# Cross-attention with layer norm: three score tiles in two TensorE visits, and a new order of the work

## Chip, core and metric

The kernel runs on one core of a Trainium2 chip. The metric is the device time of one execution in microseconds (us). A core has five engines with a queue of instructions each: TensorE (PE in the profile, with its weight loads as PEld), VectorE (DVE), ScalarE (ACT), GpSimd (POOL) and SyncE (SP), which here only issues DMA transfers.

## What is computed

Four batches of 2048 rows attend over 77 context rows each; 16 heads of 32 columns; then an output projection, a residual and a layer norm:

```
qs = (q @ wq).reshape(Bq, Lq, H, HD).transpose(0, 2, 1, 3)
ks_ = (k @ wk).reshape(Bq, Lk, H, HD).transpose(0, 2, 1, 3)
vs = (v @ wv).reshape(Bq, Lk, H, HD).transpose(0, 2, 1, 3)
scores = jnp.einsum('bhqd,bhkd->bhqk', qs, ks_) / jnp.sqrt(jnp.float32(HD))
scores = jnp.where(mask[:, None, :, :], -jnp.inf, scores)
attn_w = jax.nn.softmax(scores, axis=-1)
attn = jnp.einsum('bhqk,bhkd->bhqd', attn_w, vs)
out = attn @ wo + q
mu = jnp.mean(out, axis=-1, keepdims=True)
var = jnp.mean((out - mu) ** 2, axis=-1, keepdims=True)
return (out - mu) / jnp.sqrt(var + EPS) * gamma + beta
```

D is 512, everything is float32. q is x (8192 rows in all), k and v are the context.

## The kernel before

The 8192 rows are 64 tiles of 128 rows; two tiles make a block, four make a group. The steps of a tile, with the letter that the order uses for each:

- Q, q: one quarter of a group's query projection (12 matmuls of 512 columns, `pq`, line 177) and its copy out of PSUM (DVE, `q`, line 194). Inputs come by g (load), i (ACT cast) and j (POOL split into a high and a low part).
- S: the scores of one tile (`sc`, line 309). A head has 32 rows of contraction, so four heads run side by side in the array, and two halves of the rows too. That is 32 matmuls, which the profile shows as 64 instructions. Head h = 4g + j writes to the bank of its j, so a tile fills four PSUM banks with four blocks of 77 scores each.
- T: the maxima, in four parts of four heads. One DVE instruction for each head adds the mask, reduces and writes the negated scores to `pbuf` (line 324). Three `pbuf` take turns.
- e: the exponentials on ACT, one instruction for each head (line 339), also in four parts.
- r, n: reciprocal of the sums (DVE, line 345) and normalising (POOL, line 350).
- t: transpose in 32 x 32 blocks (DVE, line 373). P: twelve DMA transfers for each block that regroup the transposed rows, `B` to `PT` (line 385).
- V: attention of a block (`pa`, line 419); a, b: its split into a high part (ACT, line 468) and a low part (DVE, line 472).
- O: output projection of a tile (12 matmuls, `po`, line 517), + the residual (DVE, line 520), s the moments (DVE, lines 525 and 530, and on POOL the factors, lines 534 to 537), k scaling (ACT, line 543), f gamma and beta (POOL, lines 547 and 548), x and w the load of x and the store of the result.
- Once in 16 tiles: the mask of the next batch (load_mask, mask_bias, mask_min, mask_nan, lines 279 to 296).

PSUM has eight banks. They are handed out in turn (`bank`), so an instruction that writes to a bank waits until the last reader of what was there eight banks before has finished.

Nothing schedules the work: each engine runs its instructions as they are written. For tiles 0 to 53 a loop over pairs of tiles writes them. In one turn u it does S(u), O(u-6), a Q, V of block u/2-2, S(u+1), O(u-5) and another Q; from tile 54 on the words of `ORDER` are carried out one by one by `do`.

Of the kernel before, what the change touches and what calls it, by code (L numbers as in the profile page):

```python
# [8 lines left out]
F32 = mybir.dt.float32  # L9
# [4 lines left out]
ALU = mybir.AluOpType  # L14
# [3 lines left out]
P = 128  # L18
D = 512
H = 16  # L20
HD = 32
NK = 77
# [4 lines left out]
GH = 4  # L27
NG = H // GH
HEADS = [GH * g + j for j in range(GH) for g in range(NG)]
NC_D = D // P  # L30
BLK = 256
GRP = 2 * BLK
# [4 lines left out]
KSCALE = 1.0 / HD**0.5  # L37
LATE = 48
CUT = 27
HALVES = [slice(0, D // 2), slice(D // 2, D)]  # L40

ORDER = """
S54 T54.3 i31 e54.3 T54.0 O49 q58 e54.0 k47 T54.2 T54.1 +49 t53 S55 T55.0 T55.1 Q59 f47 x50 x52 T55.3 e54.2 T55.2
e54.1 j31 r54 n54 O48 q59 s49 P26.9s +48 S56 e55.0 P26.4s e55.2 e55.1 e55.3 T56.1 T56.0 P26.6g P26.0s V25 T56.2 x51
r55 a25.0 a25.1 t54 e56.1 S57 e56.2 T56.3 T57.2 Q62 P26.2g P26.8s n55 e56.3 T57.1 Q60 t55 u49 b25.0 e56.0 P26.3g Q63
e57.1 p49 e57.2 T57.3 T57.0 r56 w47 s48 b25.1 P26.5s x59 e57.3 x53 S58 P26.10s P26.7g P27.7g q62 e57.0 k46 n56 q60  # L50
P27.0s q63 u48 p48 T58.1 T58.2 P26.1s P27.1s P26.11s T58.3 e58.1 r57 t56 P27.11s n57 Q61 P27.6s f46 e58.2 T58.0 V26
q61 a26.1 t57 a26.0 x55 f48 e58.0 S59 P27.2s T59.2 P27.5s e58.3 T59.3 e59.3 P27.3s P28.4g P27.8s T59.0 O51 b26.0
P28.11g T59.1 P27.9s +51 P28.6g r58 e59.2 P28.5g O50 P27.10s b26.1 s51 e59.1 P27.4s n58 S60 Y0 u51 +50 P28.0s x57
e59.0 P28.7g P28.10s V27 T60.0 T60.1 a27.0 T60.2 a27.1 T60.3 e60.1 r59 t58 w46 P28.3s P28.9s S61 n59 O52 P28.1s
e60.3 b27.0 s50 T61.0 T61.3 t59 f49 u50 e61.0 e61.3 T61.2 b27.1 T61.1 O53 P28.8s P29.1g P29.9g e61.2 O54 S62 +52
e61.1 +53 s52 x54 r61 P28.2s V28 +54 P29.7g e60.2 x62 T62.1 T62.2 O55 p50 n61 e60.0 T62.3 x56 P29.4s r60 n60 T62.0
t61 v51 M0 P29.8s a28.0 a28.1 b28.1 b28.0 f50 t60 +55 O57 e62.2 P29.6s e62.1 P29.5s P29.10s +57 P30.6g P29.3s
P29.11s k51 P29.2s P29.0s P30.10s P30.1s e62.0 e62.3 u52 v52 S63 V29 P30.2s T63.0 P30.9s P30.5g s53 P30.7g P30.11a
s55 T63.1 r62 a29.1 P30.4s T63.3 P30.0s e63.0 P30.3s n62 b29.1 T63.2 O56 a29.0 b29.0 e63.1 I54 u53 e63.3 P30.8s s57
h63.0 y55 t62 +56 f51 O59 u55 e63.2 x58 O58 x60 k52 m63.0 y54 V30 h63.1 m63.1 I56 U62.7s U62.6s +59 J56 a30.1 u56  # L60
U62.4s U62.8s R63.0 U62.9s x61 U62.11s s59 y57 a30.0 u57 +58 u59 b30.1 b30.0 U62.5s z57 R63.1 y53 J54 R63.3 U62.1s
U62.0a R63.2 w48 E63.0a f52 w51 s58 U62.10s O60 U62.3s +60 w50 O61 U62.2a w52 y58 X63 M1 z53 E63.1a v56 v59 s60 z55
+61 y60 E63.2a u54 W62 u58 k56 E63.3a w49 w57 u60 z54 k59 c62 w54 I61 J61 W63 f56 z58 c63 d62 y61 w53 z60 w55 u61
f59 O62 w56 d63 z61 +62 s62 y62 w58 w61 w59 O63 u62 s63 z62 w60 y63 u63 w62 z63 w63
"""


# [1 line left out]
def xattn_layernorm(  # L69
# [26 lines left out]
    ring, kept, rows, summed = [], set(), {}, set()  # L96

    def bank(name):
        while len(ring) % 8 in kept:
# [196 lines left out]
        nc.vector.tensor_scalar(nz, nz, 0.0, EPS, ALU.mult, ALU.add)  # L296


    def scores(t):
        qs = qd[t // 4]  # L300
        nmax[t] = sb.tile([P, H], F32, tag="nm", bufs=3, name=f"nm_{t}")
        sums[t] = sb.tile([P, H], F32, tag="sum", bufs=3, name=f"sum_{t}")
        sc = scs[t] = [bank(f"sc_{t}_{j}") for j in range(GH)]
        for g in range(NG):
            for half in range(0, P, P // 2):
                for j in range(GH):
                    q = slice(HD * j, HD * (j + 1))
                    r0 = (t % 4) * P + half
                    nc.tensor.matmul(  # L309
                        sc[j][half : half + P // 2, g * NK : (g + 1) * NK],  # L310
                        qs[q, g, r0 : r0 + P // 2],
                        kct[q, g, t // TPB, keys_of(j)],
                        start=True,
                        stop=True,
                    )

    def maxima(t, lo, hi):
        pb = pbuf[t % NPB]
        mb = bat[t // TPB][0]
        nm = nmax[t]  # L320
        for h in HEADS[lo:hi]:
            g, j = divmod(h, GH)
            i = slot(h)
            nc.vector.tensor_tensor_reduce(  # L324
                pb[:, i // 2, (i % 2) * NK : (i % 2 + 1) * NK],
                scs[t][j][:, g * NK : (g + 1) * NK],
                mb[:, t % TPB, keys_of(h)],
                -1.0,
                3.0e38,
                ALU.add,  # L330
                ALU.min,
                accum_out=nm[:, i : i + 1],
            )

    def exps(t, lo, hi):
        pb = pbuf[t % NPB]
        for i in map(slot, HEADS[lo:hi]):
            p = pb[:, i // 2, (i % 2) * NK : (i % 2 + 1) * NK]
            nc.scalar.activation(  # L339
                p, p, AF.Exp, bias=nmax[t][:, i : i + 1], scale=-1.0, accum_out=sums[t][:, i : i + 1]  # L340
            )
# [180 lines left out]
    def moments(t):  # L522
        b, tt = divmod(t, 2)
        st = sb.tile([P, 6], F32, tag="st", bufs=3, name=f"st_{t}")
        nc.vector.bn_stats(st, od[t])
        if tt == 0:
            mvs[b] = sb.tile([P, 2, 2], F32, tag="mv", bufs=3, name=f"mv_{b}")
            rns[b] = sb.tile([P, 2, 2], F32, tag="rn", bufs=3, name=f"rn_{b}")
        mv, rn = mvs[b], rns[b]
        nc.vector.bn_aggr(mv[:, tt, :], st)  # L530
        nz = bat[t // TPB][1]
        if tt == 1:
            k = (t - 1) % TPB
            nc.gpsimd.tensor_tensor(rn[:, 0, :], mv[:, :, 1], nz[:, k : k + 2], ALU.add)
            nc.gpsimd.tensor_tensor(rn[:, 0, :], rn[:, 0, :], mhalf, ALU.pow)
            nc.gpsimd.tensor_tensor(rn[:, 1, :], mv[:, :, 0], rn[:, 0, :], ALU.mult)
            nc.gpsimd.tensor_tensor(rn[:, 1, :], rn[:, 1, :], mneg, ALU.mult)

    def scale(t):
        o = od[t]  # L540
# [170 lines left out]
        return casts.get(u) or [((u + 8) // 4, u % 4)] * (u + 8 < 4 * NGRP)  # L711

    evac = [(0, 0)]
    for u in range(0, 2 * CUT, 2):
        n = u // 2
        m, k = divmod(u, TPB)

        for q in pieces(u + 2):
            if u >= 4:
                load_xT(*q)  # L720
# [52 lines left out]
        if k == TPB - 6 and m + 1 < NB:  # L773
            load_mask(m + 1)
        if k == TPB - 4 and m + 1 < NB:
            mask_bias(m + 1)
        if k == TPB - 2 and m + 1 < NB:
            mask_min(m + 1)
            mask_nan(m + 1)

        if u:
            recip(u)
# [38 lines left out]
            q_visit(*q)  # L821
        if u >= 5:
            moments(u - 5)
        if u:
            recip(u + 1)
            normalise(u + 1)
# [5 lines left out]


    tile_ops = {
        "S": scores, "r": recip, "n": normalise, "t": transp, "W": av_tile, "x": load_x, "X": resid, "O": o_proj,
        "+": residual, "u": rsqrt_one, "y": centre, "z": finish, "k": scale, "f": affine, "w": store,
        "v": bias_one, "K": stretch, "G": shift, "p": pool_scale, "I": act_mean, "J": act_squares, "M": keep,
    }
    tile_parts = {"T": maxima, "e": exps}
    visits = {"Q": q_visit, "q": q_evac}  # L840
# [3 lines left out]
    def do(op, k, part=0, queue="s"):  # L844
        if op == "k" and k >= LATE:
            scale_one(k)
        elif op == "z" and k == NT - 1:
            finish_last(k)
        elif op == "w" and k == NT - 1:
            od.pop(k)  # L850
        elif op in tile_ops:
            tile_ops[op](k)
        elif op in tile_parts:
            tile_parts[op](k, q4 * part, q4 * part + q4)
        elif op == "s":
            (moments_one if k >= LATE else moments)(k)
        elif op in "hm":
            (recip_half if op == "h" else normalise_half)(k, part)
        elif op in visits:
            visits[op](*divmod(k, 4))  # L860
        elif op in inputs:
            inputs[op](k // 2, k % 2 * 2)
        elif op == "P":
            regroup_part(k, part, by[queue])
        elif op == "U":
            regroup_tile(k, part, by[queue])
        elif op == "R":
            flip(k, part)
        elif op == "E":
            flip_evac(k, part, nc.vector.tensor_copy if queue == "v" else nc.scalar.copy)  # L870
        elif op == "Y":
            turn_values()
        elif op == "V":
            av(k)
        elif op in "ab":
            (av_hi if op == "a" else av_lo)(k, part)
        else:
            (av_hi if op == "c" else av_lo)(k // 2, k % 2, True)

    for word in ORDER.split():  # L880
        op, (k, part) = word[0], (word[1:] + ".").split(".")[:2]
# [50 lines left out]
```

## Time and profile before

| | |
|---|---|
| median of 3 runs | 513.45 us (512.91 to 514.86) |
| profiled execution | 512.54 us, of which the span of the profile is 510.7 us |
| granted TensorE clock | 0.996 |
| busy share of the span | PE 98%, DVE 92%, ACT 92%, POOL 83% |
| DMA | 109.34 MB, mean 214 GB/s |

A row of a group gives busy time and the mean of one instruction; a row of a timeline gives start, length, engine, line, operation, output<-inputs, shape, and how many alike follow each other. Matmuls are pipelined, so starts tell more than lengths. A row of a stretch gives its length, then for each engine the busy time and how many instructions were under way.

### The profile page before, as it was taken

What the parts mean: (1) busy time and instruction counts of PE and PEld (TensorE: products, weight loads), DVE (VectorE), ACT (ScalarE), POOL (GpSimd) and SP (SyncE); (2) the same over time, 40 slices, a digit from 0 to 9 for tenths busy, and PEclk for the clock granted to TensorE, in tenths of its full rate; (3) what the DMA queues carried; (4) which work ended last, traced back from release to release, by engine and by line L of the source; (5) the groups of instructions that cost most, each with busy time, mean ns of one, the idle gap of its engine ahead of it and who ended that gap; (6) DMA issues with size and microseconds to landing.
All of it is one profiled execution on the core that took longest, in us unless ns stands there. A gap on an engine that the chain in (4) does not pass through costs nothing.

```text
span 510.7 us, 20467 instructions
## 1 busy us (share of the span) xinstructions
PE 502.1 (98%) x6864; PEld 387.3 (76%) x6864; DVE 472.1 (92%) x2574; ACT 471.2 (92%) x2239; POOL 424.3 (83%) x382
## 2 busy tenths in 40 slices
PE   8999999999999999999999999999999999999994
PEld 6987777777777777777777777777777777777784
DVE  6798999899999888989999898889999989999997
ACT  6798999999899999999899999999899999999861
POOL 0659359988799988888989998898889989999894
PEclk9999999999999999999999999999999999999998
DMA  8946867888777888789777897788887778767665
GB/s 304 400 155 150 224 177 197 217 237 221 189 207 201 233 215 224 193 222 246 185 202 218 228 230 192 181 235 230 223 217 192 211 198 234 192 185 216 166 207 207
DMA packets 58280, 109.34 MB, mean 214 GB/s; under 512 B 9203, under 2 KB 10739, under 8 KB 58176
## 3 DMA queue, kind: packets, MB, share of 16 engines
q1 hardware_dynamic: 55776, 103.19, 73.1%
q0 software_dynamic: 1872, 4.20, 2.9%
q8 instruction: 55, 0.90, 0.8%
q10 hardware_dynamic: 528, 0.66, 0.4%
q14 instruction: 49, 0.40, 0.3%
HBM read 41.53 MB, written 16.78 MB: 114 GB/s over the span
## 4 chain that ended last, share of the span: by engine, by line
PE 87%; DVE 5%; DMA 4%; SPq 2%; POOL 1%; issue 1%; ACT 1%; DVEq 0%; POOLq 0%
PE pq L177 30%; PE po L517 29%; PE pa L419 10%; PE sc L309 10%; PE sc L517 3%; DMA PT<-B 2%; DVE B L373 2%; PE pv L243 2%; PE pk L203 1%; SPq L385 1%; DVE pbuf L324 1%; DMA stage_a<-wq 1%; PE pq L669 1%; POOL pbuf L350 0%; DVE q L194 0%
## 5 line engine op out<-in xcount | busy, mean ns | idle before, releaser
L339 ACT ACTIVATE pbuf<-pbuf,nm 128x77 f32<-128x77 f32 x1024 | 352.5, 350 | 15.0 <-DVE nm L324 13.6
L339 ACT ACTIVATION_READ_ACCUMULATOR pbuf<-pbuf,nm 128x1 f32 x1024 | 195.3, 191 | 0.0
L324 DVE CUSTOM_DVE_ANT_0 pbuf<-sc,mb 128x77 f32<-128x77 f32 x1020 | 169.9, 230 | 21.8 <-PE sc L309 21.5
L350 POOL TENSOR_TENSOR pbuf<-pbuf,ri 128x1232 f32<-128x1232 f32 x63 | 142.2, 2258 | 17.8 <-DVE ri L345 11.0
L177 PE MATMUL pq<-xth,wqh 128*128 128x512 f32 (+1 forms) x256 | 98.8, 386 | 0.0
L177 PE MATMUL pq<-xtl,wqh 128*128 128x512 f32 (+1 forms) x256 | 98.0, 383 | 0.0
L177 PE MATMUL pq<-xth,wql 128*128 128x512 f32 (+1 forms) x256 | 97.9, 383 | 0.0
L373 DVE STREAM_TRANSPOSE B<-pbuf 128x1280 f32<-128x1280 f32 x63 | 93.9, 1491 | 0.3
L517 PE MATMUL po<-woh,AH 128*128 128x512 f32 x224 | 93.3, 416 | 0.0
L517 PE MATMUL po<-wol,AH 128*128 128x512 f32 x224 | 87.7, 391 | 0.0
L517 PE MATMUL po<-woh,AL 128*128 128x512 f32 x224 | 86.7, 391 | 0.0
L324 DVE DVE_READ_ACCUMULATOR2_ANT nm<- 128x1 f32 x1024 | 83.2, 81 | 0.0
L547 POOL TENSOR_TENSOR o<-o,gam 128x512 f32<-128x512 f32 x53 | 69.9, 1319 | 14.4 <-ACT o L543 14.4
L548 POOL TENSOR_TENSOR o<-o,bet 128x512 f32<-128x512 f32 x53 | 68.4, 1290 | 4.2
L309 PEld LDWEIGHTS sc<-kct,q 32*64 32x64 f32 x4080 | 51.2, 130 | 23.7 <-issue 21.3
L170 POOL TENSOR_TENSOR xtl<-xtf,xth 128x1024 fp32r<-128x1024 f32 x28 | 67.1, 2398 | 0.0
L309 PE MATMUL sc<-kct,q 32*64 32x77 f32 x4080 | 61.2, 238 | 0.0
L419 PE MATMUL pa<-PT,vsb 96*32 96x256 f32 x960 | 58.2, 382 | 0.7 <-DMA PT<-B 0.3
L177 PEld LDWEIGHTS pq<-xth,wqh 128*128 128x128 f32 x256 | 48.1, 188 | 9.8
L177 PEld LDWEIGHTS pq<-xth,wql 128*128 128x128 f32 x256 | 48.1, 188 | 9.4
L177 PEld LDWEIGHTS pq<-xtl,wqh 128*128 128x128 f32 x256 | 48.1, 188 | 9.1
L517 PEld LDWEIGHTS po<-woh,AH 128*128 128x128 f32 x224 | 42.0, 188 | 12.0 <-DVE nm L324 0.4
(167 smaller groups left out, 707.5 us busy)
## 6 DMA issues: line engine op xcount, KB each, us to landing
PT<-B SPq DMA_DIRECT2D x355, 128.0 KB
xtf<-xT SPq DMA_DIRECT2D x28, 512.0 KB
o<-x SPq DMA_DIRECT2D x56, 256.0 KB
out<-o SPq DMA_DIRECT2D x56, 256.0 KB
PT<-B POOLq DMA_DIRECT2D x16, 128.0 KB, 5.2
o_end<-x SPq DMA_DIRECT2D x7, 256.0 KB
out<-o_end SPq DMA_DIRECT2D x7, 256.0 KB
xtf<-xT SPq DMA_DIRECT2D x4, 256.0 KB
```

The lines of the kernel that those rows point to most:

```text
L170: nc.gpsimd.tensor_tensor(l, fx.pop((g, c)), h.bitcast(F32), ALU.subtract)
L177: nc.tensor.matmul(pq, w[:, c, m * P : (m + 1) * P], r[:, c, rs], start=(n == 0), stop=(n == 11))
L243: nc.tensor.matmul(pv, ctx_s[c][i][:, r, :], v[c], start=(n == 0), stop=(n == 11))
L309: nc.tensor.matmul(sc[j][half : half + P // 2, g * NK : (g + 1) * NK], qs[q, g, r0 : r0 + P // 2], kct[q, g, t // TPB, keys_of(j)], start= ...
L324: nc.vector.tensor_tensor_reduce(pb[:, i // 2, (i % 2) * NK : (i % 2 + 1) * NK], scs[t][j][:, g * NK : (g + 1) * NK], mb[:, t % TPB, keys_ ...
L339: nc.scalar.activation(p, p, AF.Exp, bias=nmax[t][:, i : i + 1], scale=-1.0, accum_out=sums[t][:, i : i + 1])
L350: nc.gpsimd.tensor_tensor(pv, pv, rv.to_broadcast((P, NP, 2, NK)), ALU.mult)
L373: nc.vector.transpose(bt.rearrange("p c q r -> p q c r"), pbuf[t % NPB].rearrange("p q (c r) -> p q c r", c=5),)
L419: nc.tensor.matmul(pas[b, g // 2][HD * j : HD * (j + 1), (g % 2) * BLK : (g % 2 + 1) * BLK], vsb[:, 2 * b // TPB, HD * h : HD * (h + 1)], ...
L517: nc.tensor.matmul(pos[t][:, cols], a[:, c, rs], w[:, c, cols], start=go, stop=done)
L547: nc.gpsimd.tensor_tensor(o, o, gam, ALU.mult)
L548: nc.gpsimd.tensor_tensor(o, o, bet, ALU.add)
```

## The change

1. From tile 12 to tile 59 the scores of three tiles (48 heads) are computed in two TensorE visits of 24 heads (Z, `scores_shared`). A visit fills four banks with six blocks of 77 scores each. Three tiles so take 8 banks and not 12.
2. The middle tile of three has its four groups of columns in two visits, so its maxima and exponentials go through the heads in another order (`SHARED`).
3. The loop ends after tile 11. From there to tile 53 the words of `STEADY` are repeated every six tiles. A word `e0.2:0:2` is: operation, tile (or visit, block, quarter) counted within six, how many repeats it lags behind, and the first repeat. The last ten tiles have a new `ORDER`. Transfers P stand apart in the order, exponentials and maxima of neighbouring tiles are mixed.
4. The POOL part of the moments becomes an operation of its own (N, `factors`), and the mask of the next batch is made after the last maxima of an odd tile (`next_mask`).

```diff
-    def scores(t):
-        qs = qd[t // 4]
-        sc = scs[t] = [bank(f"sc_{t}_{j}") for j in range(GH)]
-        for g in range(NG):
-            for half in range(0, P, P // 2):
...
+    def score_rows(cells, sc):
+        for n, (t, g) in enumerate(cells):
+            for j in range(GH):
+                scs[t, g * GH + j] = sc[j][:, n * NK : (n + 1) * NK]
             for half in range(0, P, P // 2):
                 for j in range(GH):
+                    score(t, g * GH + j, half)
+
+    def scores(t):
+        score_rows([(t, g) for g in range(NG)], [bank(f"sc_{t}_{j}") for j in range(GH)])
+
+    def scores_shared(v):
+
+        cells = [(v // 2 * 3 + n // NG, n % NG) for n in range(3 * NG)]
+        shared.add(v // 2 * 3 + 1)
+        score_rows(cells[v % 2 * 6 : v % 2 * 6 + 6], [bank(f"sz_{v}_{j}") for j in range(GH)])
+
+    def heads_of(t, lo, hi):
+        return (SHARED if t in shared else HEADS)[lo:hi]
...
-    for u in range(0, 2 * CUT, 2):
+    for u in range(0, 2 * MERGE, 2):
...
+STEADY = """
+Z0:0:2 Q1:-1:3 T0.2:0:2 T1.0:0:2 T0.1:0:2 O4:2:1 T0.0:0:2 Z1:0:2 e0.2:0:2 T1.1:0:2 i0:-2:4 Q0:-1:3 t5:1:1 e0.1:0:2
...
+    for n in range(STEADY_FROM, STEADY_TO):
+        for e, lag, first in steady:
+            b = n - lag
+            op, (k, part) = e[0], (e[1:] + ".").split(".")[:2]
+            period = 4 if op == "Z" else 3 if op in "PVabgij" else 6
+            k = int(k) + period * b
+            if b < first or k >= NT * period // 6:
+                continue
+            do(op, k, int(part or 0))
+            if op == "T" and k % 2 and part == "3":
+                next_mask(k - 1)
```

TensorE goes through the big operations of six tiles in this order: Z, Q, O, Z, Q, O, O, V, Z, O, Q, Q, O, Z, V, O, Q, Q, V, and then the next Z. Here is what stands on TensorE before the scores of tile 24 in the kernel before (`sc_24_0` to `sc_24_3` are its four banks, `pq` a query projection):

```order
L177 MATMUL pq_7_0_3472<-xtl_7_3016,wqh_67 128x512
L177 MATMUL pq_7_0_3472<-xth_7_3015,wql_68 128x512
L309 MATMUL sc_24_0_3505<-kct_71,q_6_2928 64x77
L309 MATMUL sc_24_1_3506<-kct_71,q_6_2928 64x77
L309 MATMUL sc_24_2_3507<-kct_71,q_6_2928 64x77
L309 MATMUL sc_24_3_3508<-kct_71,q_6_2928 64x77
```

And in the changed one, where `sz_16` is the visit with tile 24 and half of tile 25, and `pa_9` the attention of block 9:

```order
L198 MATMUL pq_7_1_3322<-xtl_7_2589,wqh_67 128x512
L198 MATMUL pq_7_1_3322<-xth_7_2588,wql_68 128x512
L468 MATMUL pa_9_0_3405<-PT_9_3231,vsb_72 32x256 x8
L468 MATMUL pa_9_1_3406<-PT_9_3231,vsb_72 32x256 x8
L324 MATMUL sz_16_0_3467<-kct_71,q_6_2713 64x77
L324 MATMUL sz_16_1_3468<-kct_71,q_6_2713 64x77
L324 MATMUL sz_16_2_3469<-kct_71,q_6_2713 64x77
L324 MATMUL sz_16_3_3470<-kct_71,q_6_2713 64x77
```

The attention has moved in between the projection and the scores; the visit then has 48 matmuls, not 32.

On SP, the transfers around the regrouping of blocks 14 and 15 in the kernel before (`PT_14` is block 14, `out` a store, `o_28<-x` a load of x, `xtf` a load of input):

```order
L385 DMA PT_14_4430<-B_14_4291 32x2x512 x12
L551 DMA out<-o_22_3771 128x512
L551 DMA out<-o_23_3773 128x512
L161 DMA xtf_10_2_4592<-xT 128x1024
L489 DMA o_28_4594<-x 128x512
L489 DMA o_29_4596<-x 128x512
L385 DMA PT_15_4706<-B_15_4564 32x2x512 x12
```

And in the changed one:

```order
L434 DMA PT_14_4530<-B_14_4244 32x2x512 x3
L538 DMA o_27_4704<-x 128x512
L434 DMA PT_14_4530<-B_14_4244 32x2x512 x5
L538 DMA o_26_4790<-x 128x512
L434 DMA PT_14_4530<-B_14_4244 32x2x512 x4
L434 DMA PT_15_4853<-B_15_4585 32x2x512 x5
L601 DMA out<-o_23_4251 128x512
L434 DMA PT_15_4853<-B_15_4585 32x2x512 x2
L601 DMA out<-o_21_3894 128x512
L434 DMA PT_15_4853<-B_15_4585 32x2x512 x5
```

The twelve transfers of a block stand in pieces now, with loads and stores between them; block 15 is the first of a group of three.

On ACT, before, around the split of block 11's attention (`AH_11`; `sum_27` are exponentials of tile 27, `xth` a cast of input, `o_18<-o_18` a scaling):

```order
L543 ACTIVATE o_18_3228<-o_18_3228,rn_9_3608 128x512
L543 ACTIVATE o_19_3230<-o_19_3230,rn_9_3608 128x512
L468 CAST AH_11_3923<-pa_11_0_3905 128x512
L468 CAST AH_11_3923<-pa_11_1_3906 128x512
L339 ACTIVATE pbuf0_77,sum_27_3928<-pbuf0_77,nm_27_3927 128x77 x16
L166 CAST xth_9_4105<-xtf_9_0_3769 128x1024
L339 ACTIVATE pbuf1_78,sum_28_4051<-pbuf1_78,nm_28_4050 128x77 x16
```

And in the changed one, up to the split of block 12's attention, the first block of its three:

```order
L388 ACTIVATE pbuf1_78,sum_28_3913<-pbuf1_78,nm_28_3912 128x77 x8
L388 ACTIVATE pbuf2_79,sum_29_4080<-pbuf2_79,nm_29_4079 128x77 x4
L388 ACTIVATE pbuf1_78,sum_28_3913<-pbuf1_78,nm_28_3912 128x77 x4
L388 ACTIVATE pbuf2_79,sum_29_4080<-pbuf2_79,nm_29_4079 128x77 x8
L187 CAST xth_10_4207<-xtf_10_0_4196 128x1024
L388 ACTIVATE pbuf2_79,sum_29_4080<-pbuf2_79,nm_29_4079 128x77 x4
L517 CAST AH_12_4236<-pa_12_1_4219 128x512
L517 CAST AH_12_4236<-pa_12_0_4218 128x512
```

The exponentials of two tiles are mixed in fours, and the last twelve of tile 29 stand ahead of the split. In the order's words the last three transfers of block 12 stand between the first four and the next four of these twelve, then come the cast, the last four, and V of block 12.

More of the change, by code (lines that the diff above doesn't have):

```diff
@@ L29 @@
 HEADS = [GH * g + j for j in range(GH) for g in range(NG)]
+SHARED = [GH * g + j for g0 in (0, 2) for j0 in (0, 2) for j in (j0, j0 + 1) for g in (g0, g0 + 1)
+]
 NC_D = D // P
@@ L65 @@
+c63 z55 G57 w53 f58 +62 d63 z61 w59 w55 w60 I62 J62 u62 w61 w58 y62 O63 s63 w57 y63 z62 u63 w62 z63 w63
 """
@@ L296, in mask_nan, with score @@
         nc.vector.tensor_scalar(nz, nz, 0.0, EPS, ALU.mult, ALU.add)
-    def scores(t):
-        qs = qd[t // 4]
-        nmax[t] = sb.tile([P, H], F32, tag="nm", bufs=3, name=f"nm_{t}")
-        sums[t] = sb.tile([P, H], F32, tag="sum", bufs=3, name=f"sum_{t}")
-        sc = scs[t] = [bank(f"sc_{t}_{j}") for j in range(GH)]
-        for g in range(NG):
+    def score(t, h, half):
+        g, j = divmod(h, GH)
+        q = slice(HD * j, HD * (j + 1))
+        r0 = (t % 4) * P + half
+        nc.tensor.matmul(
+            scs[t, h][half : half + P // 2],
+            qd[t // 4][q, g, r0 : r0 + P // 2],
+            kct[q, g, t // TPB, keys_of(j)],
+            start=True,
+            stop=True,
+        )
@@ L317, in maxima @@
     def maxima(t, lo, hi):
+        if t not in nmax:
+            nmax[t] = sb.tile([P, H], F32, tag="nm", bufs=3, name=f"nm_{t}")
+            sums[t] = sb.tile([P, H], F32, tag="sum", bufs=3, name=f"sum_{t}")
         pb = pbuf[t % NPB]
@@ L772, in xattn_layernorm @@
             nc.gpsimd.affine_select(unit, unit, [[-1, P]], ALU.not_equal, 1.0, base=0, channel_multiplier=1)
[L773 to L779, printed above, removed]
+        next_mask(u)
         if u:
@@ L823, in xattn_layernorm @@
             moments(u - 5)
+            factors(u - 5)
         if u:
```

108 lines of the change are left out of this document (63 added, 45 removed).

## The prediction

> **What bounds the kernel now.** I read the page first, then who waited for whom, then TensorE's timeline through the repeating middle, then busy time by stretches.
>
> ```profile
> span 510.7 us, 20467 instructions
> PE 502.1 (98%) x6864; PEld 387.3 (76%) x6864; DVE 472.1 (92%) x2574; ACT 471.2 (92%) x2239; POOL 424.3 (83%) x382
> PE 87%; DVE 5%; DMA 4%; SPq 2%; POOL 1%; issue 1%; ACT 1%; DVEq 0%; POOLq 0%
> ```
>
> TensorE is busy for 98% of the span and holds 87% of the chain that ended last. A busy matmul row can hide waiting, so the waits decide it. The first three rows are, but for one of 0.2 us, all that TensorE waited for; the fourth is its weight loader in front of a score visit.
>
> ```profile
> PE pw L638 <- POOL ident L631: 0.9, 1, 0.9
> PE pq L669 <- ACT xth L144: 0.5, 1, 0.5
> PE pa L419 <- DMA PT<-B: 0.3, 1, 0.3
> PEld sc L309 <- issue: 21.3, 56, 0.4
> ```
>
> So TensorE waits for nobody after the start: any time taken off its own instruction stream shortens the kernel, as long as the other engines keep up. The last row points at such time: 56 score visits stand behind up to 0.4 us in which the weight loader waits for nothing that the profile shows. The timeline prices it.
>
> ```profile
> 200.77 0.39 PE L177 MATMUL pq<-xth,wql 128*128 128x512 f32 x1
> 201.09 1.93 PE L419 MATMUL pa<-PT,vsb 96*32 96x256 f32 x32
> 202.95 0.95 PE L309 MATMUL sc<-kct,q 32*64 32x77 f32 x64
> 203.83 0.51 PE L517 MATMUL po<-woh,AH 128*128 128x512 f32 x1
> 204.17 0.40 PE L517 MATMUL po<-wol,AH 128*128 128x512 f32 x1
> ...
> 206.68 0.39 PE L177 MATMUL pq<-xth,wqh 128*128 128x512 f32 x1
> ...
> 209.17 0.39 PE L177 MATMUL pq<-xth,wql 128*128 128x512 f32 x1
> 209.49 0.95 PE L309 MATMUL sc<-kct,q 32*64 32x77 f32 x64
> 210.37 0.50 PE L517 MATMUL po<-woh,AH 128*128 128x512 f32 x1
> 210.71 0.39 PE L517 MATMUL po<-wol,AH 128*128 128x512 f32 x1
> ```
>
> Projections follow each other every 0.227 us: from the row at 206.68, the first of twelve, to the last at 209.17 are eleven steps. A score visit alone costs 210.71 - 209.17 = 1.54 less two steps of 0.227, so **1.09 us**. The pair of attention (pa) and scores costs 204.17 - 200.77 = 3.40 less the same, **2.95 us**. Two tiles hold 48 projections, one such pair and one lone visit: 48 x 0.227 + 1.09 + 2.95 = 14.93 us, 44.8 for six.
>
> How much of 1.09 is streaming? Cut the visit into slices of its streaming pitch:
>
> ```profile
> 209.67:209.73 0.07, 0.07 (x24) 1.00 0.56 122
> 209.73:209.80 0.07, 0.07 (x32) 1.00 1.01 217
> 209.80:209.86 0.06, 0.06 (x27) 1.00 0.95 205
> 209.48:209.86 0.38, 0.37 (x33) 1.00 0.94 216
> ```
>
> The bracketed count is of instructions under way in the slice. It grows by 8 from one slice of 0.067 us to the next, so 8.4 ns each and 0.54 us for 64. Then comes one hitch (27 in the third slice): the first half takes 0.38 us. The other 0.55 us are paid per visit, for getting into this shape of matmul and out again. The Trainium skill (TensorEngine Tiling, Key Properties) says that changing the tiling mode drains TensorE.
>
> **The change part by part.** *Score visits.* Tiles 12 to 59 now take 32 visits of 96 instructions in place of 48 of 64: the streamed work is the same, 16 visits go, and more of the rest stand beside attention, where entry and exit are shared. From tile 12 on, the old order has 24 visits alone, 22 attention-then-scores pairs, 2 scores-then-attention pairs, and 2 triples scores-attention-scores. The reverse order and the triple are in these rows:
>
> ```profile
> 429.10 0.39 PE L517 MATMUL po<-woh,AL 128*128 128x512 f32 x1
> 429.42 0.95 PE L309 MATMUL sc<-kct,q 32*64 32x77 f32 x64
> 430.45 1.93 PE L419 MATMUL pa<-PT,vsb 96*32 96x256 f32 x32
> 432.31 0.95 PE L309 MATMUL sc<-kct,q 32*64 32x77 f32 x64
> 433.20 0.50 PE L177 MATMUL pq<-xth,wqh 128*128 128x512 f32 x1
> ```
>
> A triple is 433.20 + 0.34 (the step after a change, as 203.83 to 204.17) - 429.10 - 0.45 = 3.98. A reverse pair, put together from the same rows: 0.32 to enter, 1.03 until attention starts, 1.86 until it has passed, 0.34, less 0.45: 3.1, an estimate. Old sum: 24 x 1.09 + 22 x 2.95 + 2 x 3.1 + 2 x 3.98 = 105.2 us. The new order has 9 shared and 2 plain visits alone, 15 pairs, 10 reverse pairs and one attention visit alone (3.1 - 1.09 = 2.0): 12.0 + 44.3 + 31.0 + 2.0 = 89.3, and 32 times what 32 further instructions cost. That price is not in the trace; its bounds are 32 x 8.4 ns = 0.27 us (streaming alone) and 0.38 (half a visit with hitch). I take 0.30, nearer the streaming slices, since the hitch stands once in a visit: 9.6 us. New sum 98.9, **gain 6.3 us** (7.3 at 0.27, 3.8 at 0.38).
>
> Six tiles then take TensorE about 44.8 - 0.85 = 43.9 us. *Can the others follow?* No instruction of theirs is added or removed.
>
> ```profile
> 100.00:400.00 300.00, 300.00 (x4164) 228.33 (x4164) 282.45 (x1579) 288.82 (x1382) 264.33 (x221) 1.00 0.80 214
> 420.00:440.00 20.00, 19.92 (x292) 15.73 (x291) 19.60 (x144) 19.92 (x109) 18.92 (x19) 1.00 0.71 197
> 440.00:460.00 20.00, 19.89 (x374) 14.88 (x373) 19.77 (x117) 20.00 (x108) 19.54 (x18) 1.00 0.78 204
> ```
>
> The columns are length, PE, weight loads, DVE, ACT, POOL. In 300 us ACT works 288.8 and DVE 282.5, so per 44.8 us 43.1 and 42.2: both fit into 43.9, ACT with 2% to spare. Whether engines this full can still feed TensorE is seen in the last two rows, the hand-written end of the present kernel: DVE and ACT are 98 to 100% busy there and TensorE loses 0.08 and 0.11 us of 20, 0.5%. I charge that for the eight repeats: 8 x 44 x 0.5% = **+1.8 us**, between 0 and the whole gain.
>
> *Bank release.* A PSUM bank now holds six score blocks and comes free after six reductions, not four.
>
> ```profile
> 434.79 0.15 DVE pbuf L324
> 434.95 0.15 DVE pbuf L324
> ```
>
> Reductions follow every 0.16 us. The second visit of a triple reuses the first two banks of the first; the new order reduces 16 heads (2.6 us) before that, and TensorE has a projection of Q and one of the output in between (24 x 0.227 = 5.4 us, 2.7 at the seam where only Q stands there). So it is hidden, with 0.1 us of cover at the seam, where I charge **+0.3**. If that cover goes, each visit waits for its reductions.
>
> *Splitting off the POOL factors, moving next_mask, the name SHARED:* the same instructions elsewhere, nothing. *The last ten tiles:* TensorE loses about 0.2 us in the two rows above, so there is hardly anything to win; I charge 0, within 1.5 either way.
>
> Sum: span 510.7 - 6.3 + 1.8 + 0.3 = 506.5; the profiled execution took 512.54, 1.84 more than its span: 508.3; the median of the runs lies 0.9 above that one: **509.2 us**.
>
> **The rivals.** *The longer visit is starved (511.7 us).* The hitch comes after the 32nd instruction. If TensorE has the first 32 standing ready from the projections before and must wait for every later batch of 32, as at the hitch, then each costs what the first half costs, 0.38, and the gain shrinks by 32 x 0.08 = 2.5 us. The Trainium skill (TensorE: Matmul & The Clock Gate, the table at its head) gives TensorE a queue 64 deep, just 32 weight loads with 32 matmuls; the hitch agrees with that. Against it: in the slices before the hitch 32 stream in 0.27, and nothing shows a second hitch where a visit has only 64. Chance 0.14.
>
> *ACT and DVE become the bound (513.4).* ACT's 43.1 of 43.9 leaves little, and DVE has lumps, the mask work of each batch:
>
> ```profile
> L291 DVE TENSOR_REDUCE nz<-m 128x16 f32<-128x1232 uint8 x4 | 5.7, 1417 | 0.0
> L287 DVE TENSOR_SCALAR mb<-m 128x304 bf16<-128x304 uint8 (+1 forms) x5 | 4.9, 970 | 0.0
> L286 DVE TENSOR_SCALAR mb<-m 128x1232 bf16<-128x1232 uint8 (+1 forms) x5 | 3.4, 681 | 0.0
> ```
>
> 14.0 us in four batches, 3.5 each, three of them in the changed part, against 1.7 us of DVE slack per six tiles. If each costs TensorE 1.4 us on top of the 1.8 charged, 4.2 us go back and 513.4 is left. Against it: they come in two pieces, and the slack of the next repeats takes some of it. Chance 0.12.
>
> *Slower: attention waits for its transfers (518.7).* The old order issues the 12 regrouping transfers of a block together, more than a block ahead of the attention that reads them. In the new one the first block of each three is issued in pieces, the last piece just before its attention: between them ACT has eight exponentials and one cast (8 x 0.35 + 1.04 = 3.8 us) by the first two rows here; the third is SP issuing twelve, the fourth issue to landing.
>
> ```profile
> L339 ACT ACTIVATE pbuf<-pbuf,nm 128x77 f32<-128x77 f32 x1024 | 352.5, 350 | 15.0 <-DVE nm L324 13.6
> L166 ACT CAST xth<-xtf 128x1024 fp32r<-128x1024 f32 x28 | 28.9, 1036 | 0.0
> 201.82 8.91 SPq L385 DMA_DIRECT2D PT<-B  x12
> DMA to landing us min/median/max: 3.0/5.2/6.1
> ```
>
> A landing of 5.2 would be 1.4 us late, eight times 11.2 us; 513.45 - 6.3 + 11.2 + 0.3 = 518.7. It decides from 0.8 us per repeat on, a landing of 4.6. For it: DMA is 80% busy in the middle, and SP needs 8.91 us for twelve. Against it: the data of that block are ready much earlier, so SP may be ahead of its place, and the present kernel's end has such close issues and lost 0.3. Chance 0.15.
>
> *More than forecast (505.9):* 0.27 per 32, no lost 1.8 us. Chance 0.07. The forecast keeps 0.52.
>
> **How the numbers follow.** 0.5%, 2.6 us, is about what a measurement of this kernel can tell from no change. Faster: the forecast 0.52, the better case 0.07, a third of the starved case 0.04: 0.63. Same: the rest of the starved case 0.10 and most of the engine bound 0.11: 0.21. Slower: 0.16. The range of 505.5 to 516.5 leaves out most of the slow rival and the edge of the better case; the likeliest case's own is 506.5 to 511.
>
> **What would show it.** Right: shared visits of 1.3 to 1.5 us alone; six tiles in 43.7 to 44.2; TensorE's waits below 3 us in all; ACT at 97 to 99% in the middle. Wrong: TensorE rows waiting for PT<-B (the slow rival), for reductions or exponentials (the engine bound), or a shared visit near 1.47 with the second hitch at its 64th instruction (starved).

## The result, and the profile after

| | before | after |
|---|---|---|
| median of four runs | 514.15 us (512.91 to 514.88) | 546.05 us (544.86 to 547.27) |
| profiled execution | 512.54 us, span 510.7 | 547.27 us, span 545.4 |
| granted TensorE clock | 0.996 | 0.972 |

Ratio 1.0623, 95% interval 1.0586 to 1.0661: 32 us slower where 4 us faster was forecast, and outside the range. In this part repeat n is the turn of `STEADY` that scores tiles 6n to 6n+5; n = 2 (tiles 12 to 17) is the first with scores, n = 8 the last, and the last ten tiles follow.

From the page of the kernel after, the span, the engines' busy time, TensorE's busy tenths and its clock in 40 slices, and the chain:

```profile
span 545.4 us, 20361 instructions
PE 518.9 (95%) x6864; PEld 402.0 (74%) x6864; DVE 477.7 (88%) x2573; ACT 473.0 (87%) x2245; POOL 419.6 (77%) x375
PE   8999999997899999899999989999998999998994
PEclk9999999997999999899999989999997999997998
PE 43%; ACT 17%; DVE 14%; POOL 12%; DMA 6%; issue 4%; SPq 3%; DVEq 0%; POOLq 0%; ACTq 0%
```

TensorE holds 43% of the chain, 87% before; ACT, DVE and POOL now stand in it. There are dips in TensorE's row, evenly spaced, and the clock dips at the same slices. Who waited for whom:

```profile
ACT pbuf L388 <- DVE nm L373: 20.4, 12, 2.9
ACT xth L187 <- PE pq L198: 16.9, 3, 6.3
ACT xth L187 <- DMA xtf<-xT: 7.8, 2, 6.7
...
PE sz L324 <- DVE nm L373: 4.9, 5, 2.9
PE sz L324 <- DVE q L215: 3.5, 3, 1.2
PE po L566 <- DVE o L569: 2.9, 2, 1.7
PE pa L468 <- DMA out<-o: 1.2, 1, 1.2
```

The second row is new: ACT's cast of the input waits three times, up to 6.3 us, for a query projection. TensorE's waits come to 19.7 us, 1.9 before; the last four rows are the largest of them, but for one of 1.5 us in two pieces. The timeline shows what becomes of one of ACT's waits. The rows are the starts of repeats 3 and 4, the cast in repeat 4, its stalled third score visit in three rows, and the starts of repeat 5 and of the last ten tiles:

```profile
157.81 0.32 PE L324 MATMUL sz<-kct,q 32*64 32x77 f32 x8
202.43 0.32 PE L324 MATMUL sz<-kct,q 32*64 32x77 f32 x8
213.71 1.05 ACT L187 CAST xth<-xtf 128x1024 fp32r<-128x1024 f32 x1 [6.25 <-PE pq L198]
220.90 0.60 PE L324 MATMUL sz<-kct,q 32*64 32x77 f32 x4
221.77 0.34 PE L324 MATMUL sz<-kct,q 32*64 32x77 f32 x2 [0.26 <-DVE o L569]
223.29 0.94 PE L324 MATMUL sz<-kct,q 32*64 32x77 f32 x65 [1.18 <-DVE q L215]
250.78 0.34 PE L324 MATMUL sz<-kct,q 32*64 32x77 f32 x4
444.80 0.32 PE L324 MATMUL sz<-kct,q 32*64 32x77 f32 x8
```

Repeat 3 took 44.6 us; repeat 4 took 48.35. The cast `i0` is the second item of ACT's row in a repeat and writes a buffer that `Q0` of the same repeat still reads. ACT stands for 6.25 us; the exponentials come late, DVE waits for them, and 7 us later a score visit is without its banks and its q. The query groups have four tiles and a repeat has six, so this hits every second repeat (4, 6 and 8; in repeat 2 ACT stands for 6.74 us at another cast, which waits for its load, the third row of the waits). Then the clock (columns as in the prediction, clock third from the end):

```profile
222.00:223.00 1.00, 0.11 (x2) 0.00 (x0) 0.97 (x3) 1.00 (x7) 1.00 (x2) 1.00 0.91 303
224.00:225.00 1.00, 1.00 (x54) 0.82 (x36) 1.00 (x1) 1.00 (x8) 0.26 (x2) 0.82 0.37 105
225.00:226.00 1.00, 1.00 (x4) 0.81 (x3) 0.28 (x1) 1.00 (x8) 0.00 (x0) 0.50 0.00 0
228.00:229.00 1.00, 1.00 (x6) 0.82 (x5) 1.00 (x9) 1.00 (x7) 1.00 (x1) 0.97 0.00 0
```

Behind 1.44 us of waits inside the visit the granted clock is 0.5 for 3.4 us. The kernel after has such a stretch in repeats 2, 4, 6 and 8 and in the last ten tiles; the kernel before has none until TensorE is done. In these five stretches 13.7 us of full clock are not granted. With the 17.8 us of further waits that makes 31.5 of the 34.7 us between the two spans, if all of it was paid; the rest, and the few us that the shorter stream should have saved, I can't assign.

### The profile page after: what moved, and what is told of

Same layout as the page of the kernel before. It is cut to its first block, busy times and chain, and to the rows that moved or that the text cites. A ratio compares the mean times of both kernels' runs of the same rounds, so it can differ in the third digit from the quotient of the medians.

```text
span 545.4 us, 20361 instructions
## 1 busy us (share of the span) xinstructions
PE 518.9 (95%) x6864; PEld 402.0 (74%) x6864; DVE 477.7 (88%) x2573; ACT 473.0 (87%) x2245; POOL 419.6 (77%) x375
## 4 chain that ended last, share of the span: by engine, by line
PE 43%; ACT 17%; DVE 14%; POOL 12%; DMA 6%; issue 4%; SPq 3%; DVEq 0%; POOLq 0%; ACTq 0%
PE pq L198 15%; ACT pbuf L388 14%; PE po L566 11%; PE pa L468 5%; POOL pbuf L399 5%; DVE pbuf L373 4%; PE sz L324 3%; DMA o<-x 3%; POOL o L597 2%; POOL o L598 2%; PE sc L324 2%; DVE AL L521 2%; SPq L434 2%; DVE B L422 2%; PE pv L264 2%
## 5 line engine op out<-in xcount | busy, mean ns | idle before, releaser
L373 DVE CUSTOM_DVE_ANT_0 pbuf<-sz,mb 128x77 f32<-128x77 f32 x768 | 128.1, 232 | 1.3 <-PE sz L324 0.3
L198 PE MATMUL pq<-xth,wqh 128*128 128x512 f32 (+1 forms) x256 | 100.4, 392 | 1.1 <-DVE nm L373 0.8
L566 PE MATMUL po<-woh,AH 128*128 128x512 f32 x232 | 97.7, 421 | 2.9 <-DVE o L569 2.9
L566 PE MATMUL po<-wol,AH 128*128 128x512 f32 x232 | 94.1, 406 | 0.0
L566 PE MATMUL po<-woh,AL 128*128 128x512 f32 x232 | 91.2, 402 | 0.0
L597 POOL TENSOR_TENSOR o<-o,gam 128x512 f32<-128x512 f32 x52 | 67.7, 1302 | 6.8 <-ACT o L593 5.0
L468 PE MATMUL pa<-PT,vsb 96*32 96x256 f32 x992 | 61.7, 390 | 2.1 <-DMA out<-o 1.2
L324 PEld LDWEIGHTS sz<-kct,q 32*64 32x64 f32 x3072 | 42.0, 134 | 25.6 <-issue 10.7
L324 PE MATMUL sz<-kct,q 32*64 32x77 f32 x3072 | 49.8, 244 | 10.8 <-DVE nm L373 4.9
L566 PEld LDWEIGHTS po<-woh,AH 128*128 128x128 f32 x232 | 45.8, 198 | 18.4 <-ACT AH L517 3.7
L198 PEld LDWEIGHTS pq<-xth,wqh 128*128 128x128 f32 x256 | 48.1, 188 | 12.4 <-PE pq L198 1.1
L198 PEld LDWEIGHTS pq<-xth,wql 128*128 128x128 f32 x256 | 48.1, 188 | 9.8
L198 PEld LDWEIGHTS pq<-xtl,wqh 128*128 128x128 f32 x256 | 48.1, 188 | 8.8
```

The lines of the kernel that those rows point to most:

```text
L198: nc.tensor.matmul(pq, w[:, c, m * P : (m + 1) * P], r[:, c, rs], start=(n == 0), stop=(n == 11))
L324: nc.tensor.matmul(scs[t, h][half : half + P // 2], qd[t // 4][q, g, r0 : r0 + P // 2], kct[q, g, t // TPB, keys_of(j)], start=True, stop= ...
L373: nc.vector.tensor_tensor_reduce(pb[:, i // 2, (i % 2) * NK : (i % 2 + 1) * NK], scs.pop((t, h)), mb[:, t % TPB, keys_of(h)], -1.0, 3.0e38 ...
L468: nc.tensor.matmul(pas[b, g // 2][HD * j : HD * (j + 1), (g % 2) * BLK : (g % 2 + 1) * BLK], vsb[:, 2 * b // TPB, HD * h : HD * (h + 1)], ...
L566: nc.tensor.matmul(pos[t][:, cols], a[:, c, rs], w[:, c, cols], start=go, stop=done)
L597: nc.gpsimd.tensor_tensor(o, o, gam, ALU.mult)
```

## Experiments

Times are medians, and differences are between them. Each version ran beside the kernel before, whose medians went from 512.4 to 514.2 us, so a difference below 2 us between two versions says little.

**The early cast.** E1 moves two words of `STEADY` behind V1 of the same repeat (the other words are shown without their numbers of repeats):

```
- ... T1.1 i0:-2:4 Q0 ... T1.3 j0:-2:4 e1.1 ...
+ ... T1.1 Q0 ... a1.0:1:1 i0:-2:4 Z2 n1 j0:-2:4 O0 ...
```

> The changed kernel with two words of its repeat moved: the cast i0 (and its split j0) stand after the second attention visit of the repeat, not ahead of the query projection Q0 that has to release the buffer the cast writes. Theory (the early cast blocks ACT's queue in every second repeat, TensorE then runs dry, and the granted clock halves behind that): ACT's waits for TensorE at the cast, 16.9 us, are gone, so are the half-speed stretches of repeats 2, 4, 6 and 8, and these repeats take about 44.6 us and not 48.2 to 52.6; the whole about 527 us (524 to 531). Rival A (ACT and DVE are simply too full for the shorter TensorE stream): the same time is waited for elsewhere, 540 us or more. Rival B (the regrouping transfers arrive late at the attention): no change, 546.

532.73 us, **13.3 less**, 1.7 above the range that was expected. The cast's waits for TensorE are gone from the list, repeats 4 and 6 take 44.5 and 45.3, and of the low stretches of the middle only that of repeat 2 is left. Repeats 2 and 8 still take 48.1 and 47.7. The converse puts such an early cast into the kernel before, three times:

```
+EARLY = (18, 30, 42)
-        for q in pieces(u):
+        for q in pieces(u) * (u - 2 not in EARLY) + (pieces(u + 2) if u in EARLY else []):
             cast_xT(*q)
```

(its load is moved ahead too).

> The kernel before with only the cast moved: in three turns of its loop (tiles 18, 30 and 42) the first cast of a new group is made one turn early, ahead of the query projection that still reads the buffer it writes. Theory (that place blocks ACT for some 6 us, TensorE runs dry for 2 to 3 us behind it, and the granted clock, which is 1.0 throughout the kernel before, falls to 0.5 there): 3.5 to 4 us for each, 524 us (520 to 528), with three low stretches of the clock. Rival (in an order with one tile to a visit ACT makes the wait good later): 515 us or less and no low stretch.

521.01 us, 8.6 more than before. From its waits:

```profile
ACT xth L167 <- PE pq L178: 14.4, 3, 5.4
```

So the place alone blocks ACT and costs time, 2.1, 2.1 and 3.4 us by the starts of the score visits. Only the third had a low stretch, behind a wait of attention for its transfers (1.88 us). So 5 us of blocked ACT cost TensorE 2.1 us there even without the clock; the 3.5 to 4 expected had counted the low clock in.

**The masks.** E2 leaves out the making of three masks in the kernel after, E3 does so with the cast later, f1 in the kernel before:

```
         if k == TPB - 6:
-            load_mask(m + 1)
+            bat[m + 1] = bat[m]
...
```

> The changed kernel without the making of the masks of batches 1 to 3: the rows of these batches use the mask of batch 0 (about 11 us of DVE work and three loads less). Theory (early cast): only the repeats 3, 5 and 7, in which a mask is made, get faster, by 1 to 3 us each, and the stalls of the even repeats stay: 541 us (538 to 544). Rival A (DVE's lumps make it the bound): the 11 us come back whole and more with the clock, 530 us or less.

> Both edits: the cast after the attention, and no masks made for batches 1 to 3 (they use that of batch 0). If the two causes add and nothing else holds the middle, all eight repeats take 44 to 44.8 us and the time is about 521 us (518 to 525), what is left above the 509 forecast being the tail (some 6 us), the start (2 us) and the dearer shared visits (2 us). If DVE or ACT is full anyway, repeats stay at 46 or more: 530.

> The kernel before without the making of the masks of batches 1 to 3 (their rows use the mask of batch 0). Leaving the same work out of the changed kernel gave 9 to 11 us. Theory (only the new order shows the masks' lumps of DVE work; the old one hides them in the slack of DVE): 511 to 513.5 us, at most 1.5 us gained. Rival (this work costs TensorE its time in any order, since DVE is full): 503 to 506 us.

537.25, 521.89 and 512.58 us: 8.8 and 10.8 less, and nothing (ratio 1.0002, 0.9988 to 1.0016). E2 came out below its range, but the stalls of repeats 4 and 6 stayed, as expected (48.1 and 48.0 us). E3's repeats 4 to 8 take 44.4 each. The old order hides the masks whole, the new one pays 3.6 us for each. Three ways to explain that failed. Cutting them into four pieces (f4, which also loads earlier and has the old tail), and freeing ACT or DVE elsewhere (g1, g2):

```
+        if k >= TPB - 8:                       # f4: a quarter of the biases at k = 8, 10, 12, 14
+            q0 = (k - TPB + 8) * 2
+            mask_bias(m + 1, slice(q0, q0 + 4))
...
-            do(op, k, int(part or 0))           # g1
+            if op != "k" or k % 2 == 0:
+                do(op, k, int(part or 0))
...
-        nc.vector.bn_stats(st, od[t])           # g2
+        if b not in mvs or t < 6 * STEADY_FROM:
+            sts[b] = sb.tile([P, 6], F32, tag="st", bufs=3, name=f"st_{t}")
+            nc.vector.bn_stats(sts[b], od[t])
+        st = sts[b]
```

> As the one with the old tail, and besides the mask of the next batch made in four pieces of a quarter each, two tiles apart, and its load six tiles earlier; and the input of the third repeat's casts loaded before the repeats begin. If the masks cost because they come as lumps of 1.4 to 1.7 us on DVE: 6 to 9 us less for the masks and 3 less at the seam, 515 us (511 to 519). If DVE has no room for this work in whatever pieces: only the seam's 3 us, 523 us.

> The kernel with the cast later, masks made as in the change, but in the repeats the scaling on ACT is left out for odd tiles (they are not scaled by the layer norm): about 3 x 0.7 = 2.1 us less ACT work per six tiles, TensorE and DVE unchanged. The masks cost that kernel about 11 us, spread over pieces or not. Theory A (ACT, 98% busy where no mask is made, can't make good what it loses while it waits for a maximum behind mask work): 522 to 527 us. Theory B (DVE is the one without room): 530 us or more.

> The counterpart: ACT's work is whole, but for odd tiles of the repeats the bn_stats on DVE is left out (they take the moments of the even tile): 3 x 0.67 = 2.0 us less DVE work per six tiles, 14 us in all, more than the masks of all batches take. Theory A (ACT has no room): 529 us or more. Theory B (DVE has none): 520 to 526 us.

534.94 us against 534.03 (f3 below, the same but for the masks and the load), and 533.06 and 533.48 against 532.73: nothing from any. So freeing one engine alone brings nothing. Both at once was not tried, but h3 below has all the work and repeats of 44.4 us: neither engine lacks throughput. f4 says less than its time shows, for it also has the earlier load: repeat 2 is 5.3 us shorter than in f3 (43.9 against 49.2), and repeats 4 and 7 are longer (45.7 and 49.3 against 44.3 and 45.7). So in repeats 4 to 8 the pieces cost more than the lumps. Two things were found instead. First, the place: the run without masks has gaps in DVE's row that return in every repeat, two of them about 1 us (DVE's timeline, E3, repeat 6):

```profile
305.27 0.24 DVE L368 CUSTOM_DVE_ANT_0 pbuf<-sz,mb 128x77 f32<-128x77 f32 x1 [0.91 <-PE sz L324]
316.35 0.69 DVE L564 TENSOR_TENSOR o<-po,o 128x512 f32<-128x512 f32 x1 [1.12 <-PE po L561]
```

Second, the bias itself. The groups of the narrow bias (busy time, mean ns) in the kernels before and after and in f4, and f4's timeline, POOL's row first:

```profile
L287 DVE TENSOR_SCALAR mb<-m 128x304 bf16<-128x304 uint8 x3 | 4.2, 1397 | 0.0
```

```profile
L308 DVE TENSOR_SCALAR mb<-m 128x304 bf16<-128x304 uint8 x3 | 6.3, 2094 | 0.0
```

```profile
L308 DVE TENSOR_SCALAR mb<-m 128x76 bf16<-128x76 uint8 x12 | 17.2, 1437 | 0.0
```

```profile
125.55 2.46 POOL L191 TENSOR_TENSOR xtl<-xtf,xth 128x1024 fp32r<-128x1024 f32 x1
125.70 2.38 DVE L308 TENSOR_SCALAR mb<-m 128x76 bf16<-128x76 uint8 x1
...
209.62 0.20 DVE L308 TENSOR_SCALAR mb<-m 128x76 bf16<-128x76 uint8 x1
```

A bias of 76 elements takes 0.20 us where POOL is idle and 2.38 us beside a POOL instruction, with which it ends (125.70 + 2.38 = 128.08, 125.55 + 2.46 = 128.01). So a quarter of the work waits as long as the whole, and four pieces can wait four times. The Trainium skill (SBUF — State Buffer, SBUF: two separate sides) says that DVE in a two-port mode and GpSimd share a port pair under an exclusive lock, held for a whole instruction; these rows agree. The next runs test both.

**The loads.** The base of what follows is g3, E1 with two loads earlier; g4 has the one of the tail alone. E4 is the kernel before with only the new last ten tiles, f3 is E1 with the old ones:

```
-MERGE = 6                                 # E4, with STEADY_TO = 1
+MERGE = 27
...
- x58 q61 ... x53 a26.1 ... x52 b26.1      # g4, g3
+ x58 x53 q61 ... v48 x52 ...
...
+        if u == 2 * MERGE - 2:            # g3
+            load_xT(5, 2)
-g2:-2:3
+g2:-2:4
```

> The kernel before up to tile 53 (its loop, scores of one tile in a visit), then only the new order of the last ten tiles, with the words added that the loop leaves to do (two casts, a projection, two copies) and those taken out that it has done. Theory (the tail has a stall of its own, a store of the output ahead of transfers that an attention visit needs, and a half-speed stretch behind it): 4 to 8 us slower than before, 518 to 521 us. Rival (the stall is inherited from the repeats, whose loads and stores lag): 511 to 515 us.

> The changed kernel with the cast later, and the last ten tiles in the old order with one tile to a score visit (what the loop left otherwise is put in: two output projections in place of one query projection). The new tail alone cost 5.1 us, and in the changed kernel it is some 6.6 us longer than the old tail with the same work. If that is the tail's own order: 526 us (524 to 529). If it is inherited from the repeats before it (late loads and stores): 531 to 534 us, as with the new tail.

> Of these edits the one of the tail alone: x of tiles 53 and 52 loaded earlier. Theory (DVE's residual waits for a load of x that was issued behind the transfer of the values and a dozen regrouping transfers; TensorE waits for that residual's bank, and the clock halves for some 9 us): 5 to 7 us less than with the cast later alone, 526 us (524 to 529), no low stretch of the clock in the tail. Rival (the regrouping transfers are late there whatever x does): 531 to 533 us, low stretch still there.

> The kernel with the cast later, with both edits of loads: x of tiles 53 and 52 loaded earlier in the last ten tiles, and the input of the third repeat's casts loaded before the repeats begin. Theory (the seam costs 3 to 4 us through the late load of xT, the tail 5 to 7 through the late load of x): 523 us (520 to 526). Rival (both waits are replaced by the next one): 529 to 533 us.

E4: 517.95 us, 5.1 more than before (ratio 1.0093, 1.0061 to 1.0126): the new end has a price of its own. f3: 534.03, no gain, but not the rival's proof: ACT's scaling waits 6.8 us for POOL there, behind words that I put in, a stall of its own. g4: 529.8, 2.9 less by medians that scatter by 7 us; its last ten tiles are 5.4 us shorter than E1's (88.7 against 94.1 from the first score visit to TensorE's last start) and have no low stretch. (Its middle has three low stretches, E1's one, so the whole shows less.) DVE's waits of E1 in the tail show what went:

```profile
DVE o L569 <- DMA o<-x: 3.3, 1, 3.3
```

g3: 523.29, and ACT's wait of 6.6 us for the third repeat's input is gone: both loads together are worth **9.4 us**, as expected. Repeat 2 keeps a low stretch, behind a wait of 2.49 us for maxima; a mask is made there.

**Masks again.** h1 is g3 without masks. h2 puts the masks of batches 2 and 3 into the two gaps, in halves; h3 in thirds (three places for biases, two for the minimum); the mask of batch 1 is made in the loop before the repeats. h4 adds a reordering of the last splits. i1 and i2 keep the change's places (i2 in four pieces) and alter the form: rows of an odd number of elements for the wide bias, the narrow one on ACT.

```
-            if op == "T" and k % 2 and part == "3":          # h3
-                next_mask(k - 1)
+            if 2 <= n < 8 and e in ("+1", "q2"):
+                mask_piece(n, int(e == "q2"))
...
- W62 w50 y61 J61 s60 c62 G52 u60 w54 d62 ... K57 W63 k58 ... c63 ... d63   # h4
+ W62 c62 w50 y61 J61 d62 s60 G52 u60 w54 ... W63 c63 K57 k58 d63 ...
...
+        for s in (slice(0, 7), slice(7, TPB)) if ts == slice(0, TPB) else (ts,):   # i1
+            nc.vector.tensor_scalar(mb[:, s, TAIL_K:], m8[:, s], MASKED, None, ALU.mult)
+        nc.scalar.activation(mb[:, ts, :TAIL_K], m8[:, ts, NK - TAIL_K :], AF.Copy, scale=MASKED)
```

> The cast later, the two loads earlier, and no masks made for batches 1 to 3 (they use that of batch 0). If the four causes (cast, loads at the seam, loads in the tail, masks) are the whole loss and add: 523.3 - 10.8 = 512.5 us (510 to 515), which is the kernel before: then the repeats' 0.5 us each are paid back at the ends. If something else is left: over 517.

> The same with all masks made: that of batch 1 in the loop before the repeats, those of batches 2 and 3 in halves of 0.7 to 0.9 us at the two places in a repeat where DVE was idle for 0.93 and 1.12 us. Theory (place, not amount: a lump is paid because it stands between a visit and the reductions that free its banks): 512 to 515 us, repeats of 44.4 to 44.7 throughout. Rival (any work more on DVE is paid in full): 521 to 524 us, repeats of 46 to 48 where masks are made.

> As the masks in the gaps, with the biases in thirds of some 0.7 us at three places instead of halves of 1.0 us at two. Theory (a piece is free as long as it is shorter than the gap): the two waits of TensorE for a residual (1.7 and 2.1 us between starts) go, 512 to 513.5 us, the same as before and as with no masks made. Rival (every piece costs what it takes): 516 us.

> The same, and in the last words of the order the splits of the last two tiles' attention (on ACT and DVE) stand ahead of other tiles' moments and scalings; TensorE waited for them for 0.7 and 0.6 us before its last output projections. If that wait is on the path: 1 to 1.5 us less than with the thirds alone, 511 to 512 us, 0.3% faster than before. If what was put behind is as late: no difference.

> Base: the cast later and the two loads earlier (523.3 us), masks at the places of the change. Only the form of the biases is changed: the wide one in rows of 7 and 9 tiles (an odd number of elements), the narrow one on ACT. Theory (DVE waits for a running GpSimd instruction in the other form, 1.4 to 1.9 us a batch): the two biases take 0.7 and 0.9 us on DVE each time, 2 to 5 us less, 518 to 521 us. Rival (only the lump and its place count): 523 to 525 us, since this form takes as long as the old one undisturbed.

> The same form of bias, and the mask in four pieces, two tiles apart (3, 5, 3 and 5 tiles, the minimum in halves): the cut that gave nothing in the old form. Theory: each piece now takes 0.4 to 0.6 us and is made good in the gaps of 0.3 to 1.1 us of the repeat: 513 to 517 us. Rival (the place alone counts): 521 to 525 us.

h1: 512.59 us, ratio 0.9997 (0.9971 to 1.0023). Without masks this kernel is 10.7 us faster than g3, and E3 is 10.8 faster than E1: masks and loads do add. h2: 516.11, outside both of its ranges. What was left there is in two of its rows: a half of the narrow bias in the first gap took 2.43 us, up to the end of a POOL instruction (169.55 to 172.18), and TensorE waited later for a residual from DVE:

```profile
169.85 2.43 DVE L308 TENSOR_SCALAR mb<-m 128x152 bf16<-128x152 uint8 x1
178.35 0.47 PE L573 MATMUL po<-woh,AH 128*128 128x512 f32 x1 [1.69 <-DVE o L576]
```

h3: **512.84**, ratio 0.9987 (0.997 to 1.0005), with every mask made. All of the masks' 10.5 us are recovered, by another place in DVE's row. At these places the pieces also met POOL less: the longest narrow bias took 1.49 us. Its middle, repeats 5 to 7, in one stretch:

```profile
245.00:378.00 133.00, 132.76 (x1873) 103.18 (x1873) 126.67 (x719) 130.46 (x625) 119.21 (x101) 1.00 0.77 217
```

TensorE is busy for 132.8 of 133 us, ACT for 130.5, and the clock is full. h4: 512.78, no difference: the two last waits went (0.7 and 0.6 us), and one of 1.3 us came, an attention that waits for maxima. i1: 520.93, ratio 1.0126 (1.0082 to 1.0171) against g3's 1.0216 (1.0164 to 1.0268); repeats 5 and 7 went from 47.2 and 45.9 to 44.8 and 44.4. i2: 519.8, no better than i1. So the wait of the biases for POOL was some 2 to 5 of the masks' 10.5 us (the two intervals just touch, and i1 also has the narrow bias off DVE), and cutting at the same places does not help in this form either. Rows of i2, a bias beside POOL first, then the first instruction of `mask_nan`, at two places:

```profile
124.49 0.55 DVE L312 TENSOR_SCALAR mb<-m 128x385 bf16<-128x385 uint8 x1
125.77 2.34 DVE L321 TENSOR_SCALAR nz<-nz 128x16 f32<-128x16 f32 x1
255.32 0.17 DVE L321 TENSOR_SCALAR nz<-nz 128x16 f32<-128x16 f32 x1
```

The bias no longer waits, but the two instructions of `mask_nan`, 16 elements each, still do: that of 125.77 ends with a POOL instruction (125.70 to 128.09), and its twin takes 1.19 us behind it. TensorE waits 2.67 us at 130.07, for maxima that stand behind both. The same happens again at 365 us. Repeats 2 and 8, right behind the two places, keep most of what i1 and i2 lose against h3 (i1: 44.0 and 47.2 us; h3, which makes the mask of batch 1 ahead of repeat 2: 39.5 and 44.3); repeats 5 and 6, around the place without POOL, lose 0.4 and 0.9 in i1. In h3's repeats these instructions take 0.36 us at most. So the rest of the masks' price is not shown to be the place alone: the new places also avoid POOL, and no run separates the two.

Step by step, 546.05 became 512.84: 13.3 by the cast, 9.4 by the loads, 10.5 by the masks. No version was measurably faster than the kernel before.

## Why the prediction was wrong

**What bounds the kernel held, and the visits' price came out near its upper bound.** Here is a shared visit alone, from the kernel after:

```profile
109.32 0.39 PE L198 MATMUL pq<-xth,wql 128*128 128x512 f32 x1
109.64 1.31 PE L324 MATMUL sz<-kct,q 32*64 32x77 f32 x96
110.88 0.51 PE L198 MATMUL pq<-xth,wqh 128*128 128x512 f32 x1
111.22 0.39 PE L198 MATMUL pq<-xtl,wqh 128*128 128x512 f32 x1
```

111.22 - 109.32 = 1.90, less two steps, is 1.45 us: 32 further instructions cost 0.36, not 0.30. That is the starved rival's price (0.38) all but whole, 1.9 us in 32 visits, and its sign is there: in slices of 0.067 us the count of matmuls under way falls and rises again twice in this visit (31, 19, 31, 22, 27), once in the visit of 64 (33, 19, 28). Six tiles then take 44.4 us in h3, 44.9 before (starts 104.71 to 419.07 for seven times six tiles), where the forecast had 43.9, or 44.1 with its charge of 1.8 us in eight repeats.

**"Can the others follow?": the step that failed.** It compared loads, 43.1 us of ACT's work in 43.9, charged 1.8 us, and wrote that no instruction was added. As loads that was right: h3 and E3 run at 44.4 with ACT at 98%. But here each engine works through its row in order, and what counts is where an instruction waits. The cast moved ahead of the projection that releases its buffer (13.3 us), two loads moved to just ahead of their use (9.4), the masks to places without slack and beside POOL (10.5). The term for moving `next_mask`, "the same instructions elsewhere, nothing", was the same step once more: the new places cost those 10.5 us. The order of ACT that I showed has another cast of the repeat (`i2`); I read it for the exponentials, and for no cast did I look up the buffer that it writes. The clock was not in the sum at all, up to 13.7 us.

**Last ten tiles: "0, within 1.5 either way".** The new end costs 5.1 us alone (E4), and about 1.6 us stay in h3 with the loads earlier: 415.86 to 504.93 is 89.1 us from first visit to last start, against 419.07 to 503.89, 84.8, and 2.7 for one more projection. With what repeat 3 loses (45.7 for 44.4) this returns what seven repeats gain at 0.5 each.

**Bank release and TensorE's waits.** Below 3 us of waits were expected, 19.7 came. Visits did wait for reductions and residuals that free their banks, not because six reductions stand before a release (repeat 3 has none of it), but because DVE was late.

**The rivals.** Slower was right in sign and wrong in mechanism: attention waits for a transfer once in the kernel after, for 1.2 us, in the last ten tiles. The engine bound came nearest: mask lumps are paid, at 3.6 us for each batch and not 1.4, yet not because ACT and DVE are full (g1, g2, h3). The better case's 505.9 was summed wrongly: 509.2 less 1.0 and 1.8 is 506.4.

Open stays how much of each stall is the clock's, since no run separates a wait from the low clock behind it in the new order, and how the masks' price divides between place and POOL.

## What to carry to other kernels

A sum of loads says that engines can keep up; it does not say that an order lets them. For each item that a new order moves forward, ask which buffer it writes, who still reads that, and what stands behind it in its engine's row: here one cast, 1 us of work, cost 13 us. With a repeat whose length is not a multiple of the data's groups, check every phase: repeat 3 was clean, repeat 4 was not. Work that is hidden in the old order is hidden by a gap at its place; find that gap again, and look at what runs on GpSimd beside it.

## What was not expected of the hardware

- The granted clock fell to 0.5 for 3.4 or 6.8 us behind short waits: 1.44 us inside a score visit that follows attention sufficed (repeat 4), whereas 1.14 us in such a visit (E1, repeat 8) and 2.08 us between two projections (E3) did not; 2.49 us there (g3) did. The Trainium skill (TensorE: Matmul & The Clock Gate, HAM oscillation) speaks of idle gaps over some 3.4 us; here less idle time was enough, and the lengths are one and two of such windows.
- A DVE instruction that writes 76 elements in bf16 took 0.2 us alone and up to 2.4 us beside GpSimd, ending with it, and one of 16 elements in f32 0.17 and 2.34 us; one of 385 elements in bf16 took 0.55 us beside GpSimd.
